# Plain weighted sums in layer 2's last five groups, and row sums from halves added first

## The chip, the cores and the metric

The kernel runs on one core of a Trainium2 chip. The core has five engines that run side by side and meet through semaphores: TensorE (PE, whose weight loads the profile shows apart as PEld), VectorE (DVE), ScalarE (ACT), GpSimd (POOL) and SyncE (SP). SP and POOL issue the DMAs here. Each engine works through its own list of instructions in order. Time is the device time of one launch in microseconds (us), the median of several runs; less is better.

## The reference

Four graph layers run one after the other on `x` of 2708 rows and 512 columns, each followed by `x = layernorm(x + layer(x))`. Layers 0 and 1 are not touched. Layers 2 and 3 are, cut to what matters:

```python
def _L2_gnn_ref(x, adj, weight, bias, node_w, edge_w):
    node_att = jax.nn.softmax(x @ node_w, axis=0)
    h = x @ edge_w
    e = jnp.where(adj > 0, h @ h.T, NEG_BIG)
    edge_att = jax.nn.softmax(e, axis=1)
    support = x @ weight
    return adj * (node_att * edge_att) @ support + bias

def _L3_gnn_ref(x, adj_matrix, spatial_matrix, Wq, bq, Wk, bk, Wv, bv):
    query, key, value = x @ Wq + bq, x @ Wk + bk, x @ Wv + bv
    a = query @ key.T * scale + adj_matrix + spatial_matrix
    return jax.nn.softmax(a, axis=-1) @ value
```

`adj` has about 1.2% ones. All work is in 32-bit floats. In layer 2 the scores `h @ h.T` are symmetric; in layer 3 they are not.

## The kernel before

**Tiles and groups.** The 2708 rows are 21 blocks of 128 and a last one of 20. Two blocks make a group, so there are 11 groups (`NG`), numbered 0 to 10; the last, `REMNANT`, has 128 + 20 rows. A layer of attention (`softmax_layer`, used for layers 2 and 3) treats one group of output rows `gi` at a time and steps over the groups `g` of keys and values in an order written by `key_order`: 11 x 11 = 121 steps.

**The stages of one step.** Scores are held transposed, as a tile `e` of 128 keys x 2 blocks x up to 256 outputs.

- `one_score`: a block of scores is either computed on PE (two blocks x four products of 128x256, line 1300) or, in layer 2, where `g < gi` and the mirrored block was computed before, loaded back from DRAM (`s_kept`) and turned by four PE transposes (line 1273). Scores that a later group needs are copied by ACT to `s_raw` and written to DRAM by POOL (line 1316). In the own block (`g == gi`) a quarter is copied by ACT (`s_own`) and transposed. Layer 2 masks the scores with `adj` (`masked`: ACT line 1712, DVE line 1713); layer 3 adds `2 adj` (DVE line 1794). DVE keeps a running maximum (`mx`, line 1325).
- `largest` and `spread` turn the maximum into `nmax` at a group's end (ACT line 1377).
- `begin_exp` adds `nmax` (DVE line 1383) and takes the exponential (ACT line 1384). `end_exp` adds `e` into `acc` (DVE line 1395), in layer 2 multiplies it by a second load of `adj` (`times_adj`, DVE line 1716), and forms the differences `T` (DVE lines 1402 and 1405).
- `one_sum` multiplies `e` and `T` with the values and accumulates in the four PSUM banks `po` (line 1439); `end` puts the parts together; `finish` scales by the row sums and adds the residual. Layer norm, transposes and, after layer 2, the projection to layer 3's values follow through the list `later`, one item per step.

The sums of a step run `LAG = NG + 1` = 12 steps behind its scores, so that sums of group `gi` stand beside scores of group `gi + 1`. The program order above is what the build starts from; a scheduler then lays out each engine's list.

**Seven products for eight.** The weighted sum of a step is a 2x2 block product: two blocks of outputs and two blocks of keys against two halves of 256 columns of values (`HF`). Plainly it takes eight products. The kernel before uses the Strassen-Winograd scheme, with seven: three use `e` as it is, four use the differences `t[:, 0..3]`. The values' sums stand ready: `combine(g)` writes three into `S` and writes the fourth over the second half of the group's first block, `sup[:, 2g, HF:]`:

```python
b11, b12, b21, b22 = v0[:, :HF], v0[:, HF:], v1[:, :HF], v1[:, HF:]
tt(S[:, g, 0, :], b12, b22, ALU.add)
tt(S[:, g, 2, :], b11, b12, ALU.subtract)
tt(S[:, g, 1, :], S[:, g, 0, :], b11, ALU.subtract)
tt(b12, b21, S[:, g, 1, :], ALU.subtract)
```

So after `combine` the raw half `b12` is gone. `end` (lines 1520 and 1521) adds up the four quarters from `po` into `c` with one ACT copy and seven DVE adds, before `finish2` or `finish3` reads `c`. For `gi == REMNANT` the kernel uses four products on 128 outputs and four on the 20 others (columns 128 to 147 in strips of 32), one of them with the difference `d`. The keys of the last 20 rows (`NT - 1`) stand four times in the partitions of `vals4`, once in each strip of 32, as the second factor of four short products.

**Row sums.** After the last step of a group, `row_sums` multiplies `acc` with a column of ones: two output blocks x two key blocks, one product each (line 1421), then a reciprocal.

**Between the layers.** In the stage before (from line 1590) `sup`, layer 2's values, is computed block by block and copied by ACT (line 1626), and `x2_d` is written by POOL (line 1639). While the last group of layer 2 is summed, `reload` (line 1824) brings layer 3's values into `sup` on POOL's queue, and `combine` runs again. The main loop over `t` issues `step2`, `step3`, `combine`, the reloads and `later`.

Of the kernel before, what the change touches and what calls it, by code (L numbers as in the profile page):

```python
# [8 lines left out]
F32 = mybir.dt.float32  # L9
# [8 lines left out]
P = 128  # L18
# [11 lines left out]
def gnn_stack_kernel(  # L30
# [1155 lines left out]
    x3_d = dram.tile([N, F], F32, name="x3_d")  # L1186
    v3_d = dram.tile([N, F], F32, name="v3_d")

    def key_tile(name):
# [24 lines left out]

    def softmax_layer(att, psum, later, keys, vals, query, score, weigh, load_rest, finish, mirror):

# [169 lines left out]
        def end_exp(st, k):  # L1386
# [9 lines left out]
            if weigh:  # L1396
                weigh(e[:, :, :w], load_a(gi, g)[:, :, :w])
            if g != REMNANT:
                t = att.tile([P, 2 * GROUP, P], F32, tag="T", name="T", bufs=2)
                if gi == REMNANT:  # L1400
                    d = t.rearrange("p q i -> p (q i)")[:, :w]
                    nc.vector.tensor_tensor(d, e[:, 1, :w], e[:, 0, :w], ALU.subtract)
                else:
                    q = e.rearrange("p j (i c) -> p (j i) c", c=P)
                    sub = lambda d, x, y: nc.vector.tensor_tensor(d, x, y, ALU.subtract)  # L1405
                    sub(t[:, 0:2, :], q[:, 1:4:2, :], q[:, 0:2, :])
                    sub(t[:, 2, :], q[:, 3, :], t[:, 0, :])
                    sub(t[:, 3, :], q[:, 2, :], t[:, 2, :])
                st.setdefault("t", {})[k] = t
# [3 lines left out]
        def row_sums(st):  # L1413

            gi = st["gi"]
            pr = psum.tile([P, BANK], F32, tag="tp", name="pr")
            rs = small.tile([P, GROUP], F32, tag="rs", name="rs")
            for b, it in enumerate(GROUPS[gi]):
                n = BLOCKS[it][1]
                for jb in range(GROUP):  # L1420
                    nc.tensor.matmul(
                        pr[:n, b : b + 1],
                        st["acc"][:, jb, b * P : b * P + n],
                        ones[:, 0:1],
                        start=(jb == 0),
                        stop=(jb == GROUP - 1),
                    )
                nc.vector.reciprocal(rs[:n, b : b + 1], pr[:n, b : b + 1])
            st["rs"] = rs

        def one_sum(st, k):
# [16 lines left out]
            if gi == REMNANT:  # L1448
                i = [slice(0, P), slice(w - Q, w)]
                if g != REMNANT:  # L1450
                    d = st["t"].pop(k).rearrange("p q i -> p (q i)")
                    v0, v1 = full[:, GROUP * g, :], full[:, GROUP * g + 1, :]
                    terms = [
                        (0, e[:, 0], v0[:, :HF]),
                        (0, e[:, 1], v1[:, :HF]),
                        (1, e[:, 0], S[:, g, 0, :]),
                        (1, d, v1[:, HF:]),
                    ]
                    for n, (half, x, v) in enumerate(terms):
# [19 lines left out]
                return  # L1479
            i1, i2 = slice(0, P), slice(P, GW)  # L1480
            if g == REMNANT:
                v = full[:, NT - 2, :]
# [18 lines left out]
        def end(st):  # L1501
# [3 lines left out]
            if gi == REMNANT:  # L1505
                nc.scalar.copy(c[:, 1, :HF], po[1][:, 0, :])
                picked = psum.tile([P, BANK], F32, tag="tp", name="ps_po4")
                for n in range(C):
# [7 lines left out]
                    )  # L1516
                parts = [po[0].rearrange("p h f -> p (h f)"), picked]
            else:
# [9 lines left out]
                add(at[1][0], at[1][0], po[3][:, 0, :])  # L1528
                parts = [c[:, 0, :], c[:, 1, :]]
            for b, it in enumerate(GROUPS[gi]):  # L1530
                n = BLOCKS[it][1]
                later.extend(finish(it, parts[b][:n], rs[:n, b : b + 1], r[:n, b, :]))

# [56 lines left out]
    with (  # L1590
# [7 lines left out]
        for gi, group in enumerate(PRE):  # L1598
# [16 lines left out]
            for b, it in enumerate(group):  # L1615
                i0, n = BLOCKS[it]
                ps = psum.tile([P, F], F32, tag="pr", name="ps_sup")
                for c in range(C):
# [6 lines left out]
                    )  # L1625
                nc.scalar.copy(sup[:n, it, :], ps[:n])
                xn = work.tile([P, F], F32, tag="xn", name="xn")
                nc.vector.scalar_tensor_tensor(
# [29 lines left out]

    LAG = NG + 1
    with (  # L1660
        tc.tile_pool(name="att", bufs=2) as att,
# [70 lines left out]

        def finish2(it, po, rs, y):
            i0, n = BLOCKS[it]
            nc.vector.tensor_tensor(rs, rs, natt[:n, it : it + 1], ALU.mult)
            nc.vector.scalar_tensor_tensor(y, po, rs, y, ALU.mult, ALU.add)

# [27 lines left out]
            finish2,  # L1765
            True,
        )

# [26 lines left out]

        def finish3(it, po, rs, y):
            i0, n = BLOCKS[it]
            nc.vector.scalar_tensor_tensor(y, po, rs, y, ALU.mult, ALU.add)
# [18 lines left out]
            finish3,  # L1817
            False,
        )

# [18 lines left out]
        nc.sync.dma_start(bv_sb, bv.partition_broadcast(P))  # L1839
        final = [g for g in order2(REMNANT) if g != REMNANT]  # L1840
        for t in range(start3 + steps + LAG):
# [8 lines left out]
            if t == NG:  # L1850
                combine_rest()
            k = t - (last2 - NG + 1)
            if 0 <= k < NG and order2(REMNANT)[k] != REMNANT:
# [83 lines left out]
```

## Time and profile before

| | |
|---|---|
| median of 3 runs | 3233.51 us (3231.52 to 3237.63) |
| the profiled execution: time | 3239.01 us |
| its span, from first to last instruction | 3237.0 us |
| PE: busy, share, instructions | 3168.8 us, 98%, 13448 |
| PEld | 2138.3 us, 66% |
| DVE | 2157.1 us, 67%, 3782 |
| ACT | 1347.2 us, 42% |
| POOL | 200.5 us, 6% |
| mean granted PE clock | 0.994 |
| `nmax` copies, groups 0 to 10 of layer 2 | start at 1660.4, 1724.2, 1799.9, 1871.1, 1939.7, 2007.7, 2072.6, 2136.8, 2199.2, 2264.6, 2323.6 us |
| layer 3's `nmax` copies | 2438.9, 2515.3, 2593.6, then every 78.7 to 3065.7, 3140.1, 3196.0 us |

How to read it: the profile is of one execution. Busy times are of each engine alone and overlap. Matmuls are pipelined and their ends are modelled, so a busy PE need not be a full one. Every product of 32-bit floats shows as two records of MATMUL and two of LDWEIGHTS. In a group of instructions, the columns are line, engine, operation, tiles out<-in, shapes and count, then busy us and mean ns, then the engine's idle time just before them with what ended it. In a timeline, the columns are start, length, engine, line, operation, tiles, shapes and count; in brackets, idle time before it and what ended it.

### The profile page before, as it was taken

How to read it: one execution, taken by the hardware profiler on the slowest of the kernel's cores; microseconds unless marked ns; L12 is line 12 of the kernel's file. 1: busy time of each engine (PE TensorE's matmuls, PEld its weight loads, DVE VectorE, ACT ScalarE, POOL GpSimd, SP SyncE). 2: the span in 40 equal slices, each digit the busy share in tenths (PEclk: the TensorE clock that was granted, in tenths of full speed). 3: DMA queues.
4: the chain of work that ended last, by engine and by line, in shares of the span. 5: the costliest groups of instructions: out<-in, count | busy, mean ns of one | idle time of the engine just before them, and what ended most of it. 6: DMA issues, size and time to landing. Idle time of an engine off the chain costs nothing.

```text
span 3237.0 us, 36055 instructions
## 1 busy us (share of the span) xinstructions
PE 3168.8 (98%) x13448; PEld 2138.3 (66%) x13448; DVE 2157.1 (67%) x3782; ACT 1347.2 (42%) x1464; POOL 200.5 (6%) x296
## 2 busy tenths in 40 slices
PE   8999999999999999999999999999899999999999
PEld 5444444544444446875587887777668888888886
DVE  7889987876786684444366777877844555555565
ACT  6898896477867451001133333433301111111111
POOL 1100100000000000000011111210110000000000
PEclk9999999999999999999999999999999999999999
DMA  7867865156445414541154444555441111111110
GB/s 273 308 230 244 291 234 197 44 179 214 173 171 206 146 57 123 145 107 39 46 163 126 141 129 136 166 162 154 117 125 40 49 49 49 52 49 49 49 51 29
DMA packets 208280, 429.80 MB, mean 133 GB/s; under 512 B 21866, under 2 KB 138454, under 8 KB 202282
## 3 DMA queue, kind: packets, MB, share of 16 engines
q1 hardware_dynamic: 184370, 324.15, 33.1%
q0 software_dynamic: 23296, 101.26, 8.4%
q8 instruction: 105, 1.72, 0.2%
q10 hardware_dynamic: 440, 2.10, 0.2%
q14 instruction: 69, 0.57, 0.1%
HBM read 330.07 MB, written 95.90 MB: 132 GB/s over the span
## 4 chain that ended last, share of the span: by engine, by line
PE 71%; DVE 11%; issue 10%; DMA 3%; ACT 3%; POOL 1%; SPq 0%; DVEq 0%; POOLq 0%; ACTq 0%
PE po L1439 17%; PE ps_s L1300 16%; PE po L504 14%; PE ps_nb L1156 7%; PE ps_wide L1206 4%; PE ps_sup L1619 2%; PE ps_mlp L792 2%; DVE t L416 2%; PE ps_hid L128 2%; PE ps_dec L923 2%; DVE e L1383 1%; ACT t L417 1%; DMA a_cols<-in_adjT_dram 1%; DVE a L397 1%; PE psm L541 1%
## 5 line engine op out<-in xcount | busy, mean ns | idle before, releaser
L416 DVE SCALAR_TENSOR_TENSOR t<-t,a 128x2708 f32<-128x2708 f32 (+1 forms) x152 | 450.2, 2975 | 144.9 <-ACT t L408 139.9
L408 ACT ACTIVATE t<-f1b,f2h 128x1354 f32<-128x1354 f32 (+1 forms) x304 | 415.8, 1412 | 46.7 <-PE po L504 36.3
L1439 PE MATMUL po<-sup,e 128*128 128x256 f32 (+1 forms) x1512 | 404.0, 387 | 16.7 <-DVE e L1716 13.9
L504 PE MATMUL po<-t,xw 128*128 128x452 f32 (+3 forms) x1056 | 410.4, 552 | 4.8 <-ACT t L417 4.2
L417 ACT ACTIVATE t<-t 128x2708 f32<-128x2708 f32 (+1 forms) x152 | 373.2, 2456 | 100.5 <-DVE t L416 100.2
L1300 PE MATMUL ps_s<-q,hT 128*128 128x256 f32 (+1 forms) x1848 | 405.6, 372 | 0.0
L504 PE MATMUL po<-t,emb 128*128 128x452 f32 (+3 forms) x1056 | 398.9, 546 | 3.9 <-ACT t L417 3.8
L1300 PEld LDWEIGHTS ps_s<-q,hT 128*128 128x128 f32 x1848 | 340.0, 190 | 50.4 <-issue 6.7
L504 PEld LDWEIGHTS po<-t,xw 128*128 128x128 f32 (+1 forms) x1056 | 189.6, 190 | 213.9 <-issue 193.9
L504 PEld LDWEIGHTS po<-t,emb 128*128 128x128 f32 (+1 forms) x1056 | 194.0, 191 | 201.9 <-issue 191.4
L1439 PEld LDWEIGHTS po<-sup,e 128*128 128x128 f32 (+1 forms) x1512 | 263.6, 186 | 74.1 <-issue 21.9
L1439 PE MATMUL po<-held,T 128*128 128x256 f32 x1200 | 300.9, 384 | 1.5 <-DVE T L1405 1.1
L1794 DVE SCALAR_TENSOR_TENSOR e<-a_cols,ps_s 128x512 f32<-128x512 f32 (+1 forms) x121 | 80.5, 665 | 287.2 <-PE ps_s L1300 251.6
L1439 PEld LDWEIGHTS po<-held,T 128*128 128x128 f32 x1200 | 227.8, 192 | 35.2 <-DVE T L1405 2.5
L1300 PE MATMUL ps_s<-hT 128*128 128x256 f32 (+2 forms) x968 | 215.0, 372 | 7.2 <-ACT s_own L1309 6.0
L1300 PEld LDWEIGHTS ps_s<-hT 128*128 128x128 f32 x968 | 177.0, 190 | 37.8 <-ACT s_own L1309 9.6
L1384 ACT ACTIVATE e<-e 128x512 f32<-128x512 f32 (+1 forms) x242 | 143.4, 612 | 132.6 <-DVE e L1383 131.9
L1712 ACT ACTIVATE a_cols<-a_cols,neg_big 128x512 f32<-128x512 f32 (+1 forms) x121 | 85.2, 705 | 265.0 <-DMA a_cols<-in_adjT_dram 205.4
L1156 PE MATMUL ps_nb<-hid_hi,at 128*128 128x512 f32 x484 | 185.4, 390 | 0.4 <-DVE at L1148 0.4
L1156 PE MATMUL ps_nb<-hid_lo,at 128*128 128x512 f32 x462 | 179.9, 389 | 0.0
L1383 DVE TENSOR_TENSOR e<-e,nmax 128x512 f32<-128x512 f32 (+1 forms) x242 | 154.0, 666 | 18.0 <-ACT nmax L1377 16.6
L1786 ACT ACTIVATE q<-ps_wide,uq 128x256 f32<-128x256 f32 (+1 forms) x44 | 20.5, 466 | 332.9 <-PE ps_wide L1206 332.9
(267 smaller groups left out, 4046.8 us busy)
## 6 DMA issues: line engine op xcount, KB each, us to landing
a_cols<-in_adjT_dram SPq DMA_DIRECT2D x300, 256.0 KB
a<-adj_d SPq DMA_DIRECT2D x108, 677.0 KB
a<-in_adjT_dram SPq DMA_DIRECT2D x42, 677.0 KB
adj_d<-a POOLq DMA_DIRECT2D x42, 677.0 KB, 5.5
kept<-t POOLq DMA_DIRECT2D x20, 1354.0 KB, 6.8
t<-kept SPq DMA_DIRECT2D x20, 1354.0 KB
raw<-in_adjT_dram SPq DMA_DIRECT2D x105, 256.0 KB
scores<-s_raw POOLq DMA_DIRECT2D x45, 256.0 KB, 3.2
```

What stands on the lines that cost most here:

```text
L408: tanh = nc.scalar.activation(tv[:, k, :], f1b[k][:n, :w], AF.Tanh, bias=f2h[:n, jt, h : h + 1], scale=0.5,)
L416: step = nc.vector.scalar_tensor_tensor(tv, tv, GUARD, ab, ALU.add, ALU.mult)
L417: exp = nc.scalar.activation(tv, tv, AF.Exp, scale=0.5)
L504: nc.tensor.matmul(po[HB * k + q][:, :qw], values[r : r + n, jt, h * P : (h + 1) * P], t[r : r + n, k, q0 : q0 + qw], start=(place == 0), ...
L1156: nc.tensor.matmul(pos[it][:n], at, half[:, jt, :], start=(jt == 0 and k == 0), stop=(jt == NT - 1),)
L1206: nc.tensor.matmul(ps[:, :width], w(c, o), xt(c), start=(c == 0), stop=(c == C - 1),)
L1300: nc.tensor.matmul(ps[:, jb, i:w], keys[:, c, j : j + P], st["q"][:, c, i:], start=(c == 0), stop=(c == C - 1),)
L1383: nc.vector.tensor_tensor(e, e, nm, ALU.add)
L1384: nc.scalar.activation(e, e, AF.Exp)
L1439: nc.tensor.matmul(po[bank][rows, half, :], lhsT, rhs, start=(k == 0 and half == 0) if first is None else first, stop=last, skip_group_che ...
L1712: nc.scalar.activation(a, a, AF.Identity, bias=neg_big[: a.shape[0]], scale=1.0e30)
L1794: nc.vector.scalar_tensor_tensor(e, a, 2.0, ps, ALU.mult, ALU.add)
```

## The change

Three things change.

1. From group 6 of layer 2 on (`PLAIN_FROM = 6`; layer 3 gets `NG`, so never) the weighted sums are plain. `end_exp` forms no `T`. `one_sum` makes eight products per step, each of the four quarters in the first half of its own bank of `po`; `end` adds nothing, and `finish` reads the two halves of a block from two banks, through the new `add_up`. The short products of the last 20 rows use the strips 0, 1, 2 and again 0 of `vals4`. Group 10 keeps its eight products and no longer forms `d`.
2. The plain sums need the raw half `b12`. It is written to DRAM (`v2_d`) on POOL's queue when it is computed, for groups 0 to 9, and loaded back on POOL's queue during the steps in which group 5, the last with the seven products, is summed, each half after its last use there.
3. In both layers `row_sums` first adds the two key halves of `acc` on DVE and then makes one product per output block.

```diff
             if weigh:
                 weigh(e[:, :, :w], load_a(gi, g)[:, :, :w])
-            if g != REMNANT:
+            if g != REMNANT and gi < plain_from:
                 t = att.tile([P, 2 * GROUP, P], F32, tag="T", name="T", bufs=2)
...
             gi = st["gi"]
+            w = GSPAN[gi][1]
+            acc = st["acc"]
+            nc.vector.tensor_tensor(acc[:, 0, :w], acc[:, 0, :w], acc[:, 1, :w], ALU.add)
             pr = psum.tile([P, BANK], F32, tag="tp", name="pr")
...
-                for jb in range(GROUP):
-                    nc.tensor.matmul(
-                        pr[:n, b : b + 1],
-                        st["acc"][:, jb, b * P : b * P + n],
-                        ones[:, 0:1],
-                        start=(jb == 0),
-                        stop=(jb == GROUP - 1),
-                    )
+                nc.tensor.matmul(
+                    pr[:n, b : b + 1],
+                    acc[:, 0, b * P : b * P + n],
+                    ones[:, 0:1],
+                    start=True,
+                    stop=True,
+                )
...
-                    d = st["t"].pop(k).rearrange("p q i -> p (q i)")
                     v0, v1 = full[:, GROUP * g, :], full[:, GROUP * g + 1, :]
-                    terms = [
-                        (0, e[:, 0], v0[:, :HF]),
-                        (0, e[:, 1], v1[:, :HF]),
-                        (1, e[:, 0], S[:, g, 0, :]),
-                        (1, d, v1[:, HF:]),
-                    ]
+                    terms = [(0, e[:, 0], v0[:, :HF]), (0, e[:, 1], v1[:, :HF])]
+                    if gi < plain_from:
+                        d = st["t"].pop(k).rearrange("p q i -> p (q i)")
+                        terms += [(1, e[:, 0], S[:, g, 0, :]), (1, d, v1[:, HF:])]
+                    else:
+                        terms += [(1, e[:, 0], v0[:, HF:]), (1, e[:, 1], v1[:, HF:])]
...
             i1, i2 = slice(0, P), slice(P, GW)
+            if gi >= plain_from:
+                for jb, jt in enumerate(GROUPS[g]):
+                    if jt != NT - 1:
+                        for b, i in enumerate((i1, i2)):
+                            for h in range(2):
+                                product(
+                                    2 * b + h,
+                                    0,
+                                    e[:, jb, i],
+                                    full[:, jt, h * HF : (h + 1) * HF],
+                                    first=(k == 0 and jb == 0),
+                                )
+                        continue
+                    for n, bank, i in ((0, 0, i1), (1, 1, i1), (2, 3, i2), (0, 2, i2)):
+                        own = slice(n * Q, n * Q + REST)
+                        product(bank, 0, e[own, 1, i], vals4[own])
+                return
...
-                parts = [po[0].rearrange("p h f -> p (h f)"), picked]
+                parts = [[po[0].rearrange("p h f -> p (h f)")], [picked]]
+            elif gi >= plain_from:
+                parts = [[po[2 * b + h][:, 0, :] for h in range(2)] for b in range(GROUP)]
...
-                parts = [c[:, 0, :], c[:, 1, :]]
+                parts = [[c[:, 0, :]], [c[:, 1, :]]]
...
                 nc.scalar.copy(sup[:n, it, :], ps[:n])
+                if it % GROUP == 0 and it < NT - GROUP:
+                    nc.gpsimd.dma_start(v2_d[:, it // GROUP, :], sup[:, it, HF:])
...
-        def finish2(it, po, rs, y):
+        def add_up(parts, rs, y):
+
+            w = F // len(parts)
+            for k, x in enumerate(parts):
+                own = y[:, k * w : (k + 1) * w]
+                nc.vector.scalar_tensor_tensor(own, x, rs, own, ALU.mult, ALU.add)
+
+        def finish2(it, parts, rs, y):
             i0, n = BLOCKS[it]
             nc.vector.tensor_tensor(rs, rs, natt[:n, it : it + 1], ALU.mult)
-            nc.vector.scalar_tensor_tensor(y, po, rs, y, ALU.mult, ALU.add)
+            add_up(parts, rs, y)
...
+            k = t - (PLAIN_FROM * NG - NG + LAG)
+            if 0 <= k < NG and order2(PLAIN_FROM - 1)[k] != REMNANT:
+                g = order2(PLAIN_FROM - 1)[k]
+                nc.gpsimd.dma_start(sup[:, GROUP * g, HF:], v2_d[:, g, :])
```

`finish3` changes in the same way as `finish2`.

More of the change, by code (lines that the diff above doesn't have):

```diff
@@ L1187, in gnn_stack_kernel @@
     v3_d = dram.tile([N, F], F32, name="v3_d")
+    v2_d = dram.tile([P, NG - 1, HF], F32, name="v2_d")
     def key_tile(name):
@@ L1213, in project_wide, with softmax_layer @@
             put(o, ps[:, :width])
-    def softmax_layer(att, psum, later, keys, vals, query, score, weigh, load_rest, finish, mirror):
+    def softmax_layer(
+        att, psum, later, keys, vals, query, score, weigh, load_rest, finish, mirror, plain_from
+    ):
         full, S, apart, vals4, po = vals
@@ L1528, in end @@
                 add(at[1][0], at[1][0], po[3][:, 0, :])
-                parts = [c[:, 0, :], c[:, 1, :]]
+                parts = [[c[:, 0, :]], [c[:, 1, :]]]
             for b, it in enumerate(GROUPS[gi]):
                 n = BLOCKS[it][1]
-                later.extend(finish(it, parts[b][:n], rs[:n, b : b + 1], r[:n, b, :]))
+                later.extend(
+                    finish(it, [x[:n] for x in parts[b]], rs[:n, b : b + 1], r[:n, b, :])
+                )
         states = {}
@@ L1659, in gnn_stack_kernel @@
     LAG = NG + 1
+    PLAIN_FROM = 6
     with (
@@ L1766, in gnn_stack_kernel @@
             True,
+            PLAIN_FROM,
         )
@@ L1794, in biased, with finish3 @@
             nc.vector.scalar_tensor_tensor(e, a, 2.0, ps, ALU.mult, ALU.add)
-        def finish3(it, po, rs, y):
+        def finish3(it, parts, rs, y):
             i0, n = BLOCKS[it]
-            nc.vector.scalar_tensor_tensor(y, po, rs, y, ALU.mult, ALU.add)
+            add_up(parts, rs, y)
             def rest():
@@ L1818, in gnn_stack_kernel @@
             False,
+            NG,
         )
@@ L1839, in gnn_stack_kernel @@
         nc.sync.dma_start(bv_sb, bv.partition_broadcast(P))
-        final = [g for g in order2(REMNANT) if g != REMNANT]
         for t in range(start3 + steps + LAG):
```

## The prediction

> **What bounds the kernel.** I began with the page (PE busy 98%, DVE 67%, PE 71% of the chain that ended last) and then cut the time where layers 2 and 3 run into stretches. Each stretch below runs from one group's `nmax` copy (ACT L1377) to the next: in it one group of layer 2 has its weighted sums and the next its scores. The first three rows are the sums of groups 1 to 3, the next four those of groups 6 to 9 (the change begins at 6), the last is a group of layer 3. After the length come, for PE, PEld, DVE, ACT and POOL, busy time and records, then PE clock, DMA share and GB/s.
>
> ```profile
> core 0: us, PE busy (x) PEld busy (x) DVE busy (x) ACT busy (x) POOL busy (x), PEclk, DMA share, GB/s
> 1724.20:1799.90 75.70, 74.21 (x348) 59.64 (x349) 53.17 (x114) 27.46 (x44) 11.22 (x15) 1.00 0.44 130
> 1799.90:1871.10 71.20, 70.52 (x336) 57.09 (x337) 52.19 (x114) 26.76 (x44) 10.27 (x14) 1.00 0.48 138
> 1871.10:1939.70 68.60, 67.65 (x324) 54.41 (x324) 51.42 (x114) 25.93 (x42) 12.88 (x13) 1.00 0.48 143
> ...
> 2072.60:2136.80 64.20, 59.57 (x288) 47.02 (x287) 50.85 (x113) 24.34 (x40) 9.28 (x10) 1.00 0.53 154
> 2136.80:2199.20 62.40, 57.91 (x276) 45.53 (x275) 50.37 (x113) 24.03 (x38) 7.97 (x9) 0.97 0.56 157
> 2199.20:2264.60 65.40, 59.96 (x264) 44.66 (x264) 51.53 (x112) 23.41 (x37) 6.67 (x8) 0.92 0.56 161
> 2264.60:2323.60 59.00, 54.98 (x249) 40.34 (x249) 46.84 (x115) 19.20 (x34) 5.17 (x6) 0.97 0.43 117
> ...
> 2672.30:2751.00 78.70, 78.70 (x380) 68.26 (x379) 43.43 (x101) 12.68 (x23) 1.08 (x2) 1.00 0.19 50
> ```
>
> PE's records fall from 348 to 249, yet the stretches stop shrinking at 64 us, while DVE stays near 51. Busy time does not say how full PE is, since matmul ends are modelled. So I priced PE's work where it is dense, by the chain of waits in a group of layer 3 (start, us, work; a product of 256 columns is two records):
>
> ```profile
> 2704.60 3.02 PE po L1439 x14
> ...
> 2713.57 3.45 PE ps_s L1300 x16
> 2717.02 2.37 PE po L1439 x16
> ...
> 2735.99 0.34 PE pr L1421 x4
> ```
>
> Seven products take 3.02 us, so one takes 0.431; a computed score step takes 3.45, the remnant's sums 2.37, the row sums of one block 0.34. The timeline of layer 2 adds 0.44 for a score step of four transposes (L1273). **PE's need** in the stretch of group 8's sums: ten sums 30.2 + remnant 2.37 + row sums 0.68 + two finished blocks, each 0.44 of transposes and 3.43 of projection, 7.7 + largest and spread 0.65 + scores of group 9 (nine transposed 4.0, own block 2.75 for four products, four halves and a transpose, remnant 2.73) = 51.1 us. One more computed step in place of a transposed one is +3.0, so groups 7 and 6 need 54.1 and 57.1, group 5 60.1, group 4 63.1, and groups 3, 2, 1 need 66.1, 69.2, 72.2 (groups 4 and 5 took 68.0 and 64.9). Group 9, whose neighbour's scores are 148 columns wide, needs about 48. **Slack** (length less need) is 3.5, 2.0 and 2.5 in groups 1 to 3, about 4.9 in 4 and 5, then 7.1, 8.3, 14.3 and 11.0. It grows as DVE's busy time comes up to PE's need: 0.74 to 0.78 of it in groups 1 to 3, 0.89, 0.93, 1.01, 0.98 in groups 6 to 9. Layer 3's group has a need of 78 in 78.7: none.
>
> What PE waits for, by the timeline, here in group 8 (brackets: idle time and what ended it):
>
> ```profile
> 2210.09 1.65 PE L1439 MATMUL po<-sup,e 128*128 128x256 f32 x6 [1.93 <-DVE e L1716]
> ...
> 2248.40 1.58 PE L1300 MATMUL ps_s<-hT 128*128 128x128 f32 x8 [1.96 <-ACT s_own L1309]
> ```
>
> At a group's start DVE runs the seven adds of `end`, two `finish` operations, T's subtractions and the layer norm without a gap (2199.6 to 2210), and PE waits for the weighted `e` queued among them (2.34 us at the start of groups 6 and 7). Later it waits some 2 us per group for `s_own`, on an ACT held up by loads of `a` and by DVE.
>
> **The change, part by part.** DVE first, by the groups of the stretch 2199 to 2265:
>
> ```profile
> L1405 DVE TENSOR_TENSOR T<-e,T 128x128 f32<-128x128 f32 x20 | 5.7, 283 | 0.3
> L1405 DVE TENSOR_TENSOR T<-e 128x256 f32<-128x256 f32 x10 | 5.6, 565 | 3.2 <-PE po L1439 2.9 <-DMA v_d<-v 0.3
> ...
> L1520 DVE TENSOR_TENSOR c<-c,po 128x256 f32<-128x256 f32 x7 | 2.8, 415 | 0.0
> ```
>
> - *Removed on DVE* in groups 6 to 9: 30 subtractions (10.4 to 11.3 us as recorded; neighbours overlap by some 0.1, so 9.4) and the seven adds (2.3 so counted); also one ACT copy of 0.37. `finish` reads PSUM in four pieces: 4 x 0.415, by the add that reads po, against 2 x 0.748: +0.2. The new half-sum is 128x256, like `mx<-mx` at 0.41. Net -11 us: DVE falls to about 40, 0.65 to 0.73 of PE's new need.
> - *Added on PE*: one product more per step, 10 x 0.431 = 4.31 us per group. The remnant's four 20-row products have two on the same rows: +0.2, bounds 0 and 0.43. Row sums: one `pr` product per block, 0.34 less per group. New needs: 61.3, 58.3, 55.3, 52.2 (+4.17 each).
> - *What slack is left* is the step that decides, and the trace doesn't show it. Bounds: 2.0, the best of groups 1 to 3; and today's values, the product paid in full (4 x 4.17 = +16.7 us). I take 3.5, the upper of groups 1 to 3, since DVE will stand below their ratio while DMA is busier here (0.53 to 0.56 against 0.44 to 0.48). Lengths: 64.8, 61.8, 58.8, 55.7; against 64.2, 62.4, 65.4, 59.0 that is +0.6, -0.6, -6.6, -3.3: **-9.9 us**. The lower bound gives -15.9.
> - *Group 10* has as many products as before, without its subtraction, and group 9's banks come free after one DVE operation each. The waits that this touches are `T` L1402 1.60 and `c` L1520 1.06 and 0.20: **-2.0**, bounds 0 and -4. `s_own` or `a` is late next.
> - *Row sums elsewhere*, 7 groups of layer 2 and 11 of layer 3: 18 x 0.34 = 6.1 at most. Of this 5.2 is taken, as part of layer 2's falls into existing waits: **-5.2**. The added wait: `pr` now waits for one more DVE operation, and the next sums stand behind `pr` on PE. In layer 3 DVE had been idle 2.81 us when it started at 2814.73, and `pr` began at 2814.53: an add of 0.41 fits. Without that cover it costs 0.4 to 1.1 (the add, and one 128x512 operation in front) per group, +20 over 18 groups at worst; no row suggests it.
> - *Saved and reloaded halves*: ten writes of 128 KB in front of x2's writes on POOL's queue, which idles 20 us between triples there; ten loads while group 5 sums, 0.55 to 0.72 us of issue each, 7 us on a POOL busy 10.4 of 64.9. A reload waits in that queue for PE's last product with the block; behind it stand score stores (four `x` buffers) of later steps. Each lands ten steps, some 55 us, ahead of its use; such loads took 3 to 5 us. 1.3 MB on 9.7 MB of that stretch delay some loads of `a`: **+0.5**, bounds 0 and +3.
>
> Sum: -9.9 - 2.0 - 5.2 + 0.5 = -16.6 us on the profiled execution's 3239.0 (span 3237.0 and 2.0 around it), or -0.51%; on the median of 3233.5 that is **3217 us**.
>
> **Two rules against these rows.** The Trainium skill, *Perfetto Trace Analysis*, "Identifying the Most-Contended Engine", says to take the engine with the highest occupancy and relieve it first. That is PE in every stretch, and the change loads it. By this rule groups 6 to 9 cost +16.7. By the rows the slack there is 7 to 14 us, against 2 to 3.5 where DVE has room, and the sum is -9.9. I follow the rows, as PE's waits name DVE. *TensorE: Matmul & The Clock Gate*, Part 1, puts half clock after a full idle window of about 3.4 us. No wait found in these stretches is that long, so by the rule the clock costs nothing; but the rows grant 0.97, 0.92 and 0.97 in groups 7 to 9, worth 1.7 + 5.1 + 1.7 = 8.5 us, and 1.00 in groups 1 to 3 and 6. I count this as part of slack that goes with the waits; if it stayed, -9.9 would become -1.4.
>
> **Rivals.**
> - *The waits stay, fed by loads (slower).* ACT waited 19 to 27 us for `a_cols` in each of the stretches of groups 6 to 8, DVE 3.5 to 6.3; if these loads, four buffers deep, pace `e` and `s_own`, freeing DVE moves nothing and PE pays +16.7: 16.7 - 2 - 5.2 + 0.5 = +10, **3243**. It decides as soon as slack stays above 7.7 on average (today 10.2). Against it: PE's first waits end with DVE operations in an unbroken DVE run.
> - *A draw in groups 6 to 9*: slack falls by just the 4.17 added; -6.7, **3227**.
> - *Denser still*: slack 2.0, group 10 -4, all row sums -6.1: -26, **3207**.
> - *The change does not take*: sums of group 6 wait for reloads. Excluded by the ten steps above.
>
> **Chances.** Forecast 0.50, draw 0.20, denser 0.16, slower 0.14. Under 0.2% (6.5 us) I call no change: about what repeats of this kernel can tell. The draw sits on that edge and is split; a little of the forecast's tail goes to no change: faster 0.72, same 0.14, slower 0.14. Range 3203 to 3238: it leaves out the slower rival's upper part and a tail below; the forecast alone spans 3208 to 3226.
>
> **What will show it.** Right: stretches of groups 6 to 9 at 65, 62, 59, 56 with clock near 1.00, DVE near 40, no PE wait above 1 us on `e` L1716 at group starts, layer 3's groups shorter by 0.34. Wrong: PE still waiting 2 us there or for `s_own`; waits before `pr`; `sup` reloads as releasers; group 6 longer by 2 us or more.

## The result and the profile after

| | before | after |
|---|---|---|
| median of 14 runs each, on one chip | 3232.44 us (3229.89 to 3237.63) | 3224.77 us (3220.62 to 3231.76) |
| ratio of the times, 95% interval | | 0.9977 (0.9969 to 0.9985), -7.4 us |
| first profiled execution: time | 3239.01 us | 3230.21 us |
| second profiled execution: time (span) | 3230.14 us (3228.0) | 3225.45 us (3223.7) |

Faster, as forecast, but by less than half: 16.6 us were predicted. The profile that the prediction was made from is of a long execution, 6.6 us above the median of its kernel. Both kernels were therefore profiled once more. These second executions differ by 4.7 us in time, and they are compared here.

The stretches of the changed kernel, second execution, cut at the same `nmax` copies as in the prediction (length, then busy time and records of PE, PEld, DVE, ACT and POOL, then PE clock, DMA share, GB/s). The first four rows are the sums of groups 6 to 9, the fifth is group 10 up to layer 3's first `nmax`, the last is a group of layer 3.

```profile
core 0: us, PE busy (x) PEld busy (x) DVE busy (x) ACT busy (x) POOL busy (x), PEclk, DMA share, GB/s
2069.70:2137.90 68.20, 64.09 (x302) 51.52 (x301) 43.98 (x84) 23.76 (x38) 8.86 (x11) 0.97 0.49 146
2137.90:2199.50 61.60, 59.52 (x294) 48.05 (x293) 41.73 (x79) 21.19 (x36) 8.97 (x9) 1.00 0.53 161
2199.50:2258.10 58.60, 57.07 (x281) 45.21 (x280) 41.27 (x78) 22.47 (x37) 12.03 (x8) 1.00 0.59 178
2258.10:2319.30 61.20, 58.43 (x265) 43.99 (x263) 36.56 (x81) 19.05 (x32) 5.71 (x6) 0.97 0.40 113
2319.30:2430.40 111.10, 106.95 (x510) 76.16 (x510) 55.45 (x135) 20.66 (x39) 20.54 (x29) 0.98 0.40 118
...
2662.30:2740.60 78.30, 78.30 (x376) 67.88 (x375) 43.83 (x102) 12.67 (x23) 1.08 (x2) 1.00 0.18 50
```

Groups 6 to 9 of the unchanged kernel, second execution:

```profile
2069.80:2133.70 63.90, 59.58 (x289) 47.02 (x288) 50.84 (x113) 24.33 (x39) 9.26 (x10) 1.00 0.52 152
2133.70:2196.20 62.50, 58.00 (x276) 45.61 (x276) 50.37 (x113) 23.99 (x38) 7.96 (x9) 0.97 0.54 159
2196.20:2258.30 62.10, 55.53 (x265) 41.74 (x264) 51.05 (x112) 23.45 (x38) 8.37 (x8) 1.00 0.57 168
2258.30:2314.70 56.40, 54.70 (x249) 40.31 (x248) 46.62 (x115) 19.39 (x34) 5.16 (x6) 0.97 0.44 123
```

DVE's busy time fell by 6.9, 8.6, 9.8 and 10.1 us in groups 6 to 9, to between 41 and 44 in groups 6 to 8 and 36.6 in group 9. Forecast were some 11 us less and about 40. (At the start of group 6 DVE still runs the seven adds for group 5.) PE got its extra product (PEld rises by 2.4 to 4.5 us a group). But the lengths went +4.3, -0.9, -3.5, +4.8. What became longer and shorter, by the two second executions (us):

| | groups 0 to 5 | groups 6 to 9 | group 10 | layer 3, ten stretches | sum |
|---|---|---|---|---|---|
| before | 411.4 | 244.8 | 115.3 | 757.1 | |
| after | 407.9 | 249.7 | 111.1 | 752.6 | |
| difference | -3.5 | +4.9 | -4.2 | -4.5 | -7.3 |
| forecast, by its own base | part of -5.2 | -9.9 | -2.0 | part of -5.2 | |

These parts sum to -7.3, but the two spans differ by 4.3 only. What lies before group 0's `nmax`, which the change leaves alone but for the ten writes, took 1661.8 us against 1658.4 (in the first pair 1660.1 and 1660.4), and the rest after layer 3's last `nmax` gave back 0.3. So it is by chance that the sum meets the -7.4 of the medians.

Layer 3's value is the same in both profiles of each kernel, to 0.1 us: in all 18 traces of this document it is 757.1 us with the old row sums and 752.6 with the new ones. Group 10 is nearly as firm: 115.3 to 119.5 us in the four traces where it has the difference `d`, 109.6 to 113.9 in the 14 where it has plain sums. The others vary: groups 6 to 9 took 251.0 and 244.8 in the two executions of before, 253.2 and 249.7 in those of after. So their difference lies between -1.3 and +8.4, and in no pairing near -9.9. Groups 0 to 5 took 412.2 and 411.4 before, 411.8 and 407.9 after, so their -3.5 is loose as well.

What PE, DVE and ACT waited for in groups 6 to 9 (waiting line, releaser, us in total, times, longest us); first before, then after, second executions:

```profile
DVE e L1716 <- DMA a_cols<-in_adjT_dram: 14.3, 12, 2.3
PE po L1439 <- DVE e L1716: 6.8, 4, 2.3
PE ps_s L1300 <- ACT s_own L1309: 5.2, 3, 2.1
```

```profile
ACT a_cols L1742 <- DMA a_cols<-in_adjT_dram: 87.2, 25, 8.9
DVE e L1746 <- DMA a_cols<-in_adjT_dram: 26.7, 17, 3.2
PE ps_s L1303 <- ACT s_own L1312: 6.2, 3, 2.7
PE ps_s L1297 <- ACT e L1296: 2.8, 1, 2.8
PE po L1444 <- DVE e L1746: 1.4, 2, 0.8
```

PE's wait for the weighted `e` at the starts of groups is gone, from 6.8 to 1.4 us, and so are its waits for `T` (2.5 before). In their place DVE waits longer for loads of `a`, and PE still waits for two small copies by ACT, `s_own` and the remnant's partial scores, 9.0 us in all against 6.3 before. Why those are late is seen in the timeline, here at the end of group 9 (start, length, engine, line, operation; in brackets idle time and what ended it):

```profile
2289.50 0.54 ACT L1742 ACTIVATE a_cols<-a_cols,neg_big 128x296 f32<-128x296 f32 x1 [3.79 <-DMA a_cols<-in_adjT_dram]
2289.94 0.26 ACT L1296 COPY e<-ps_parts 128x148 f32<-128x148 f32 x1
2290.26 0.52 PE L1297 MATMUL ps_s<-e,quarters 128*128 128x148 f32 x2 [2.77 <-ACT e L1296]
```

The mask of this step stands in front of the copy in ACT's list and waits 3.79 us for its load of `a`. The copy needs only PE's result, but it starts 0.44 us after the mask, and PE waits 2.77 us for a copy of 0.26 us. This wait is one for a load, and not for a busy DVE. DVE still has an indirect part: in these four stretches the loads of `a` stood 42.1 us in SP's queue until a DVE mask (L1743) and 28.6 us until a DVE product (L1746) was done, 26.3 us until an earlier load had landed; and loads of mirrored scores, issued from the same queue, stood 35.3 us there until PE was done with their buffer. The trace does not part these from each other.

### The profile page after: what moved, and what is told of

Same layout as the page of the kernel before. It is cut to its first block, busy times and chain, and to the rows that moved or that the text cites. A ratio compares the mean times of both kernels' runs of the same rounds, so it can differ in the third digit from the quotient of the medians.

```text
span 3228.4 us, 35961 instructions
## 1 busy us (share of the span) xinstructions
PE 3169.6 (98%) x13440; PEld 2144.0 (66%) x13440; DVE 2122.0 (66%) x3654; ACT 1345.5 (42%) x1460; POOL 212.2 (7%) x316
## 5 line engine op out<-in xcount | busy, mean ns | idle before, releaser
L1444 PE MATMUL po<-sup,e 128*128 128x256 f32 (+1 forms) x2000 | 497.4, 386 | 8.1 <-DVE e L1746 6.6
L1444 PEld LDWEIGHTS po<-sup,e 128*128 128x128 f32 (+1 forms) x2000 | 348.4, 185 | 77.1 <-issue 22.4
L1303 PEld LDWEIGHTS ps_s<-q,hT 128*128 128x128 f32 x1848 | 340.0, 190 | 50.4 <-issue 6.7
L1444 PE MATMUL po<-held,T 128*128 128x256 f32 x960 | 240.2, 384 | 0.9 <-DVE T L1408 0.8
L1444 PEld LDWEIGHTS po<-held,T 128*128 128x128 f32 x960 | 182.3, 192 | 28.1 <-DVE T L1408 2.7
```

The lines of the kernel that those rows point to most:

```text
L1303: nc.tensor.matmul(ps[:, jb, i:w], keys[:, c, j : j + P], st["q"][:, c, i:], start=(c == 0), stop=(c == C - 1),)
L1444: nc.tensor.matmul(po[bank][rows, half, :], lhsT, rhs, start=(k == 0 and half == 0) if first is None else first, stop=last, skip_group_che ...
```

## The experiments

Ratios are to the kernel before on the same chip, with their 95% intervals; the chips differ between runs. "+" and "-" in the cuts of code are against the changed kernel. "Slack" is length less PE's need, with the prediction's needs. Lengths of stretches and sums of waits are each from one profiled execution.

### Each part alone

**Row sums alone**: `PLAIN_FROM` = `NG`, and `v2_d` neither written nor read.

```diff
-    PLAIN_FROM = 6
+    PLAIN_FROM = NG
```

> The row sums alone, with the seven products kept in every group and no saved or reloaded half. Theory A (the row sums carry most of the measured gain, and the plain sums in groups 6 to 10 about break even): layer 3's groups shorter by 0.44 us each as in the changed kernel, layer 2's first groups by 0 to 0.4, so 5 to 7 us in all, ratio about 0.998. Theory B (the plain sums carry the gain and the row sums only what layer 3 shows): 4 to 5 us from layer 3 and nothing or a loss in layer 2, ratio 0.9985 to 0.999.

Measured 0.9982 (0.9976 to 0.9989), -5.8 us. Layer 3 took 752.6 us as in the changed kernel; group 10 took 115.5, as before the change.

**Plain sums alone**: the row sums as they were.

```diff
-            nc.vector.tensor_tensor(acc[:, 0, :w], acc[:, 0, :w], acc[:, 1, :w], ALU.add)
...
+                for jb in range(GROUP):
+                    nc.tensor.matmul(
+                        pr[:n, b : b + 1],
+                        acc[:, jb, b * P : b * P + n],
```

> The plain sums from group 6 on with their saved and reloaded halves, with the row sums of the kernel before. Theory A: 0 to 3 us gained, ratio 0.999 to 1.000; group 6 some 5 us longer than before, group 8 some 4 shorter, group 10 some 5 shorter. Theory B: 4 us or more gained, ratio 0.9985 or less.

Measured 1.0015 (1.0006 to 1.0023), +4.8 us over the kernel before: a loss, which neither expectation had. Layer 3 is back at 757.1; groups 6 to 9 took 254.0, group 10 111.1.

What follows: the row sums carry most of the gain. The plain sums alone lose; beside the new row sums (0.9977 against 0.9982) they neither gain nor lose anything that can be told. Group 10's -4 us belongs to the plain sums. One thing does not fit: the parts alone give -5.8 + 4.8 = -1.0 us, together they give -7.4. By the three intervals this difference of 6.4 us is uncertain by some 4, so most of it may be chance; what is left of it is unexplained.

**The halves' traffic**: the ten writes and the ten reloads left out. In this kernel the plain sums of groups 6 to 10 use the combined half where the raw one belongs, so this part of the values is changed; every product is still made.

```diff
-                if it % GROUP == 0 and it < NT - GROUP:
-                    nc.gpsimd.dma_start(v2_d[:, it // GROUP, :], sup[:, it, HF:])
...
-                nc.gpsimd.dma_start(sup[:, GROUP * g, HF:], v2_d[:, g, :])
```

> The changed kernel without the ten writes and ten reloads of the raw half; the plain sums of groups 6 to 10 then multiply with the combined half in its place. The forecast's price for this traffic was 0.5 us, at most 3. Group 5's stretch, 66.0 us with it, would fall to 65.0; ratio 0.9973 to 0.9976. If the traffic disturbs the loads of a more than thought: 3 us or more better than the changed kernel.

Measured 0.9967 (0.9956 to 0.9978). That is 3 us less than the changed kernel, but the intervals overlap. Group 5, beside whose sums the reloads run, took 64.9 us against 66.0 and 65.0 in the two profiles with them.

### Where the plain sums begin

> Plain sums from group 7 on. Theory A (group 6 pays the added products since its slack was least, 7.1 us): group 6 back at about 64 us, the others as in the changed kernel, so 5 us better than the changed kernel, 12 to 13 us better than before, ratio 0.996. Theory C (the loss lies in one late load in front of an ACT copy and falls where the order of the loads puts it, whichever group is first): group 6 or 7 stays some 4 us long and the time is within 2 us of the changed kernel, ratio 0.9975.

> Plain sums from group 8 on. Theory A: groups 6 and 7 as before the change, group 8 some 4 us shorter than before, group 10 some 5 shorter, row sums 5 to 7: 13 us better than before, ratio 0.996. Theory C: a group stays long by some 4 us, ratio 0.9975.

> Plain sums in group 10 alone, where they add no product, with the new row sums. If group 10 is where the plain sums gain (its stretch was 110.0 us against 115.4) and groups 6 to 9 pay more than they get: row sums 5.8 and group 10 some 5 us, ratio 0.9965, better than the changed kernel by 3 to 4 us. If groups 6 to 9 bring the gain: no better than the row sums alone, 0.9980 to 0.9985.

Each is one edit, `PLAIN_FROM` = 7, 8 or 10. Measured 0.9969 (0.9957 to 0.9982), 0.9979 (0.9969 to 0.9988) and 0.9971 (0.9961 to 0.9982); from 6 it was 0.9977. Where they begin cannot be told by time. With 7, group 6 (now with seven products) took 63.5 us and not 68 to 70, but group 7, now the first plain one, took 64.5 and not 61.5 or 61.8: part of the length moved along. With 10, groups 6 to 9 have seven products as before the change and took 243.6, and group 10 still has its gain, at 111.9 (115.3 before). So four groups of plain sums gain nothing that shows, and group 10 some 3 to 4 us. In the profiled executions the four groups even lose: 253.2 and 249.7 us in the changed kernel, against 243.9 (row sums alone) and 243.6 with seven products. The medians do not show this loss, so how large it is stays open.

### The small copies and the loads, one at a time

**Copies on DVE.** In layer 2 `s_own` and the remnant's partial scores are copied by DVE, which has room now.

```diff
-                        nc.scalar.copy(e[:, 1, :w], parts[:, :w])
+                        (nc.vector.tensor_copy if mirror else nc.scalar.copy)(e[:, 1, :w], parts[:, :w])
...
-                        nc.scalar.copy(s[:, 0, :P], ps[:, 0, P:])
+                        nc.vector.tensor_copy(s[:, 0, :P], ps[:, 0, P:])
```

> The changed kernel with layer 2's two small copies that PE waits for (s_own of the own block, and the remnant's partial scores) on DVE in place of ACT. Theory D (they stand in ACT's queue behind a mask that waits for a late load of a, and PE waits for them): the waits of 3.3, 2.5, 2.2 and 3.4 us in groups 6 to 9 shrink below 1 us, half-clock pieces there go; 8 to 12 us better than the changed kernel, ratio to before about 0.9945. Theory E (PE waits because the late load itself is needed a little later, whatever engine copies): the waits move to the next score step; within 2 us of the changed kernel, ratio 0.9975.

**A fifth buffer for `a`.**

```diff
-            a = att.tile([P, GROUP, GW], F32, tag="a", name="a_cols", bufs=4)
+            a = att.tile([P, GROUP, GW], F32, tag="a", name="a_cols", bufs=5)
```

> The changed kernel with five buffers for the loaded columns of adj in place of four. Theory D and E (the load is late since its buffer comes free late): loads start a step earlier, ACT's waits for them fall by half, PE's waits for the two copies shrink; 5 to 10 us better than the changed kernel, ratio about 0.9955. Theory F (the load is late since it stands in SP's queue behind the reload of mirrored scores, which waits for its own buffer, or since DMA is slow): little change, within 2 us, ratio 0.9975.

**Mirrored scores on another queue**, so that they no longer stand among the loads of `a` in SP's queue.

```diff
-                    nc.sync.dma_start(dst, src)
+                    nc.gpsimd.dma_start(dst, src)
```

> The changed kernel with the reloads of mirrored scores on POOL's queue in place of SP's. Theory F: loads of a no longer stand behind them; ACT's waits for a_cols and PE's waits for the two copies shrink; 4 to 8 us better than the changed kernel, ratio 0.9960. If buffers alone make the loads late: within 2 us, or a loss of a few us where mirrored scores now stand behind POOL's other work.

Measured 0.9967 (0.9955 to 0.9979), 0.9974 (0.9963 to 0.9986), 0.9968 (0.9956 to 0.9980): each 1 to 3 us below the changed kernel by its middle value, none told apart from it, and none with the 4 to 12 us that the reading behind it had. The timeline of the first of them in group 7, with the copy on DVE:

```profile
2168.02 0.69 DVE L1746 TENSOR_TENSOR e<-e,a_cols 128x512 f32<-128x512 f32 x1 [1.85 <-DMA a_cols<-in_adjT_dram]
2168.63 0.28 DVE L1312 COPY s_own<-ps_s 128x128 f32<-128x128 f32 x1
...
2168.97 1.16 PE L1303 MATMUL ps_s<-hT 128*128 128x128 f32 x8 [3.02 <-DVE s_own L1312]
```

The copy now stands behind a DVE operation that waits for `a`, and PE waits 3.02 us for it, in a group that had met its forecast. In the last of the three, by PE's waits in groups 6 to 9 (columns as above):

```profile
PE ps_s L1303 <- ACT s_own L1312: 9.7, 3, 5.1
```

Here one wait for the copy on ACT took 5.1 us. In these two the wait changes its engine or its group and stays. With five buffers the waits for `s_own` stayed too (6.3 us in groups 6 to 9), but the wait for the remnant's copy and the half clock were gone, and groups 6 to 9 took 243.2 us, a mean slack of 4.0. That profile is of the shortest of its eight executions, and the median shows no such gain.

**All three together:**

> The changed kernel with all three reliefs: the two small copies on DVE, a fifth buffer for the loaded columns, and mirrored scores reloaded on POOL's queue. Theory H: loads come earlier and fewer waits stand behind them; slack of groups 6 to 9 near 4 us, 8 to 10 us better than the changed kernel, ratio to before about 0.995. If the reliefs only move the waits: as each alone, 0.9967 to 0.9970.

Measured 0.9985 (0.9978 to 0.9993): worse than either expectation and, if anything, than each alone; groups 6 to 9 took 252.0.

**From group 10 with the remedies.** Plain sums in group 10 only, with copies on DVE and five buffers:

> The run before with the two small copies on DVE and a fifth buffer for the loaded columns. PE's waits for these copies are some 2 us in each of groups 6 to 9 with the seven products; where half of that goes it is 4 us better than the run before, ratio 0.995 to 0.9955. Where DVE, fuller here than with plain sums, delays the copies: no better than the run before, 0.9965.

and in group 10 only, with the mirrored scores on POOL's queue:

> Plain sums in group 10 alone, new row sums, and mirrored scores reloaded on POOL's queue. Theory H (with seven products DVE paces groups 6 to 9): no more than 3 us better than without the moved reloads, ratio 0.9962 to 0.9972. If SP's queue is what holds the loads in either plan: 4 us or more better, 0.996 or less.

Measured 0.9978 (0.9971 to 0.9984) and 0.9981 (0.9973 to 0.9989), neither better than plain sums in group 10 alone. No version of the whole computation that was tried is faster than the changed kernel beyond its interval.

### Half the loads

The sharpest test of what holds the slack up. From group 6 on, the multiplication of `e` by `adj` takes a resident tile of ones instead of the second load of `adj`: the operation stays on DVE, the load goes. What these two kernels leave out is the factor `adj` in groups 6 to 10. First with plain sums, then with seven products and the new row sums.

```diff
-                weigh(e[:, :, :w], load_a(gi, g)[:, :, :w])
+                weigh(e[:, :, :w], (load_a(gi, g) if gi < 6 else ones_a)[:, :, :w])
```

> The changed kernel, but in groups 6 to 10 of layer 2 the second multiplication by adj takes a tile of ones that stays in SBUF, so that its load goes and the DVE operation stays. Theory H (freeing DVE was worth only half of the forecast because loads of a, not DVE, then release e and hold ACT): with half the loads the slack of groups 6 to 9 falls from 7 us on average to the 3.5 that was forecast, some 14 us better than the changed kernel, ratio to before about 0.9935, and better than the next run by 5 us or more. Theory G (PE is as full as it gets and the added products are simply paid): within 4 us of the changed kernel, and not better than the next run.

> The row sums alone with the seven products kept, and the same tile of ones in place of the second load in groups 6 to 10. Theory H: DVE still paces these groups, so little is gained over the row sums alone, 0 to 6 us; ratio 0.9965 to 0.998. Theory G: loads were what PE waited for here too, 6 us or more gained, ratio 0.996 or less, and better than the run before.

Measured 0.9953 (0.9941 to 0.9966) and 0.9956 (0.9942 to 0.9970). The stretches of groups 6 to 9 with plain sums and half the loads:

```profile
2072.50:2137.20 64.70, 62.45 (x302) 50.10 (x302) 43.33 (x83) 24.03 (x38) 9.35 (x11) 1.00 0.36 110
2137.20:2198.10 60.90, 59.44 (x293) 47.98 (x292) 41.26 (x78) 20.94 (x35) 8.98 (x9) 1.00 0.37 115
2198.10:2255.20 57.10, 57.08 (x281) 45.26 (x281) 40.52 (x78) 22.90 (x37) 12.05 (x8) 1.00 0.42 130
2255.20:2311.60 56.40, 56.40 (x265) 42.99 (x264) 35.97 (x80) 18.06 (x31) 5.41 (x6) 1.00 0.29 84
```

DVE's busy time is as in the changed kernel, PE's products are the same, only the DMA share fell (0.53 to 0.37 in group 7). PE shows busy from end to end in groups 8 and 9, at full clock, and the slack is 3.4, 2.6, 1.8 and 4.2, on average 3.0: what the prediction had taken as 3.5. So the second loads, with the buffers and the places in the queue that they take, are what stood between the forecast's slack and the measured one.

The two kernels also part PE's waits by their cause. Seven products with half the loads, then plain sums with half the loads, in groups 6 to 9 (columns as above):

```profile
PE po L1444 <- DVE e L1746: 7.6, 5, 2.3
PE ps_s L1303 <- ACT s_own L1312: 1.8, 3, 1.0
```

```profile
PE ps_s L1304 <- ACT s_own L1313: 2.2, 2, 1.4
PE po L1445 <- DVE e L1749: 1.4, 2, 0.8
```

With all loads these waits were 7.6 and 5.8 us with seven products (row sums alone), 1.4 and 6.2 with plain sums. So the wait for DVE's weighted `e` goes with the plain sums, whatever is loaded, and the wait for `s_own` goes with the loads, whatever the products are.

In time, the same relief helps seven products as much: 8.4 us against row sums alone, 7.7 us for plain sums against the changed kernel. The reading that plain sums would win by 5 us or more once loads are out of the way missed: they are 1 us apart. So did the readings in which half the loads give little, in either kernel. Where seven products gained their 8.4 us is not seen. Their profile is of the longest of five executions (3221.45 us, median 3216.73); groups 6 to 9 took 240.2 in it, against 239.1 with plain sums, but group 10 took 119.5 against 115.5 with row sums alone.

### The two second profiles

> The kernel before, unchanged, for a second profile. Theory J (the first profiled execution was unusual in groups 6 to 9): their four stretches sum to 245 to 248 us in place of 251.0, with less than 10 us of half clock in place of 17.1. Against it: 250 us or more, with 14 us or more of half clock.

> The changed kernel, unchanged, for a second profile. Theory J: group 6 near 66 us in place of 70.0, groups 6 to 9 at 246 to 249 in place of 253.2. Against it: group 6 at 69 us or more again.

Single executions of the two kernels without any edit, 3230.14 and 3225.45 us; their rows are in the section on the result. For the kernel before, the reading that its first execution was long in groups 6 to 9 held (244.8 us, 6.8 at half clock). For the changed kernel neither reading did: group 6 at 68.2 and groups 6 to 9 at 249.7 lie between them.

## Why the prediction was right in sign and wrong in size

**What bounds the kernel: right.** PE in layer 3 and in groups 1 to 5, and PE held up by DVE at the starts of groups 6 to 9. The relief took 8.8 us a group off DVE on average, where 11 were forecast, and those waits went: 6.8 us to 1.4, while with seven products and half the loads they stayed at 7.6.

**PE's needs: right in groups 6 to 8, too low in group 9.** With half the loads PE shows busy 62.5, 59.4 and 57.1 us in groups 6 to 8, 1.1 to 1.8 above the needs; its ends are modelled, so this is as near as the profile tells. In group 9 it was busy for all of 56.4 us, at full clock, against a need of 52.2. Most of the difference is in the nine score steps with four transposes, two of them of 20 columns. Here is one, with what follows on PE:

```profile
2287.11 0.86 PE L1277 MATMUL ps_s<-ident,s_kept 128*128 128x128 f32 x4
2287.90 3.72 PE L1445 MATMUL po<-sup,e 128*128 128x256 f32 x16
```

Such a step holds PE for 0.79 us, and 0.44 was taken, the price in the other groups: nine times 0.35 is 3.2 us. The forecast's length of group 9, 55.7, was less than PE's own work.

**What slack is left: the step that failed.** The prediction took 3.5 us for each of groups 6 to 9, and -9.9 us in all. The second profiles show +4.9. Three terms of it were off.

1. *The base.* The lengths from which 9.9 is reckoned come from one execution, whose groups 6 to 9 took 251.0 us with 17.1 us at half clock. The second took 244.8 with 6.8. So about 6.2 of the 9.9 us belonged to that execution and were not there to be gained. The prediction set its sum against the execution's own time and then carried it over to the median unchanged.
2. *PE's need in group 9*, too low by 4.2, as above.
3. *The slack itself.* Length less the prediction's need was 6.9, 3.3, 3.3 and 9.0, on average 5.6 (8.7, 3.5, 6.1 and 7.8 in the first profile after). With group 9's need put right it was 4.8 there, and 18.3 in all where 14 were taken: 4.3 more. Of that 3.4 is in group 6, where PE's wait for `s_own`, behind a mask that waits for its load, stayed (2.7 us), and with it a piece of half clock.

Together -9.9 + 6.2 + 4.2 + 4.3 = +4.8 us. What the third term had wrong is the cause of the slack: the ratio of DVE to PE was taken as what sets it. DVE now stands at 0.70 to 0.75 of PE's new need, about as the 0.74 to 0.78 of groups 1 to 3, and group 6 has 6.9 us and not 2.0 to 3.5. The text of the prediction had the counter-evidence, ACT waiting 19 to 27 us per group for `a`, and named `s_own` as held up "by loads of `a` and by DVE", but let the whole wait go with DVE. The runs with half the loads show that this wait is one for loads. The prediction's own signs of being wrong came with it: PE waited over 2 us for `s_own`, and group 6 was longer by 4.3.

That the total still came out on the right side is due to the row sums and group 10, not to groups 6 to 9, where the forecast had most of its gain.

**The rival "the waits stay, fed by loads".** Right about the waits for `s_own` and the remnant's copy, as halving the loads shows; wrong about the waits at the starts of groups, which went with DVE's work. It was to decide above a slack of 7.7; 5.6 stayed, so its +16.7 became about +4.9 in those groups, and the total stayed below zero. The draw, 3227, is nearest to what came, but not by its sum: it had nothing lost in groups 6 to 9 and less gained in group 10.

**Group 10: right in sign, too small.** -4.2 for -2.0, just past the bound of -4. PE's idle time in it (length less busy) fell from 8.1 to 4.2 us, nearly all of the gain.

**Row sums: right.** -5.8 us alone (-3.6 to -7.8), for 6.6 forecast with those in groups 6 to 9. A group of layer 3 became shorter by 0.45 us, not 0.34. The added wait of `pr` for one more DVE operation cost nothing that shows.

**Saved and reloaded halves: right.** +0.5 was taken, 0 to 3 as bounds; leaving them out (0.9967 against 0.9977) changed no more than the intervals leave open. Each reload landed in 2.3 to 4.7 us, for 3 to 5 taken, and no instruction waited for one.

**The two rules.** The Trainium skill, *Perfetto Trace Analysis*, "Identifying the Most-Contended Engine", takes the engine with the highest occupancy, but judges TensorE by matmul work done and by the busy share of LDWEIGHTS, not by that of matmuls. The prediction applied it by matmuls and found PE. By LDWEIGHTS it finds DVE in groups 6 to 9 of the kernel before: PEld 47.0, 45.6, 41.7 and 40.3 us against DVE's 50.8, 50.4, 51.1 and 46.6. So by that measure the rule spoke for this change there, as the rows did, and in groups 6 to 9 relieving DVE did not pay all the same: the product given to PE and the waits for loads took it up. In group 10, where PE's work stays the same, it paid. For *TensorE: Matmul & The Clock Gate*, Part 1, see the last section: the half clock did not go with DVE's waits, it was 6.8 us in groups 6 to 9 in both second executions.

**What stays open**: whether the two parts together really are better than their sum; how much of the late loads is transfer, how much buffers and how much place in the queue; and whether the best order of loads on SP's queue would give plain sums their slack. An order of loads written anew was not tried.

## What to carry to other kernels

Before a gain is taken from idle time, read that idle time in a second execution: here about 6 of 10 us were of one execution. When an engine is relieved, ask of each wait which instruction stands *in front* of the releaser in its queue and what that one waits for; a copy of 0.3 us behind an operation waiting for a load is a wait for the load. Price a step by its own shapes: four transposes, two of them of 20 columns, took 0.79 us and not 0.44. The parts that took work from PE or left it as it was (row sums, group 10) gained about what was forecast or more; the part that bought DVE time with PE time gained nothing that shows.

## What was not expected of the hardware

PE runs at half clock for pieces of 3.4, 6.8 or, twice, 10.2 us, nearly always after waits shorter than 3.4 us. Two waits of the kernel before, first execution, at the starts of groups 6 and 7:

```profile
2082.24 1.56 PE L1439 MATMUL po<-sup,e 128*128 128x256 f32 x6 [2.34 <-DVE e L1716]
...
2146.44 2.82 PE L1439 MATMUL po<-sup,e 128*128 128x256 f32 x6 [2.35 <-DVE e L1716]
```

The waits are alike, but the same six records took 1.56 us after the first and 2.82 after the second. The granted clock (columns as in the stretches; it stands behind POOL) was 1.00 after the first wait and 0.50 after the second:

```profile
2078.31:2081.72 3.41, 1.59 (x8) 1.06 (x6) 3.41 (x9) 0.68 (x2) 0.00 (x0) 1.00 0.29 77
2081.72:2085.14 3.41, 2.89 (x20) 2.08 (x20) 3.41 (x9) 2.49 (x4) 0.37 (x1) 1.00 0.32 80
2143.16:2146.58 3.41, 1.07 (x6) 0.61 (x5) 3.41 (x9) 1.34 (x2) 0.00 (x0) 1.00 0.19 65
2146.58:2149.99 3.41, 3.41 (x9) 2.56 (x10) 3.41 (x10) 1.41 (x3) 0.00 (x0) 0.50 0.28 77
```

These windows are not chosen at will. In layers 2 and 3 of each of the 18 traces the half-clock pieces begin at whole multiples of 3.413 us from one another. Laid out on this grid, all 44 full-clock windows in which PE shows busy for less than 1.4 us were followed by half clock, 16 of 26 with 1.4 to 1.6 us, and 7 of 7579 with more. So it is not the length of a wait that decides here, but how much of one window it empties: the first wait is spread over two windows and leaves 1.59 us in the emptier one, the second lies almost whole in one window and leaves 1.07. A wait of 3.42 us in the kernel with five buffers brought no half clock at all. The rule weighed in the prediction, half clock only after a whole idle window of about 3.4 us, would have given none after these two waits.

A wait that is caught so costs itself and up to half of the piece after it, by an estimate from these clocks 1.7 us for each window of 3.4. Half clock in groups 6 to 9 came to anything from 0 us (five buffers; no reloads; plain sums with half the loads) to 23.9 us (plain sums from group 10 with mirrored scores on POOL's queue). It is one reason why two executions of the same kernel differ by 6 us in four stretches: there 17.1 and 6.8 us of half clock account for some 5 at most.
